# Four graph layers on one core: one chunk of edges in some units fetched row by row by SyncE

## The chip, the cores and the metric

The kernel runs on one core of a Trainium2 chip, as one program. Its time is device time in microseconds (us), from start to end of one execution. Engines are named as in the profile: PE is TensorE, DVE is VectorE, ACT is ScalarE, POOL is GpSimd, SP is SyncE, which does no arithmetic on tiles: it issues DMAs, loads registers and waits. "SPq" and "POOLq" are the sequencers' own instructions.

## The reference, cut to what matters

A graph of 12,500 nodes with 128 features and 212,500 edges, sorted by their target node `dst`, passes through four layers, each added to its input `x`. Every layer reads, for each edge, the row of its source node `src`, and reduces over the edges of a target.

```python
h = relu(layernorm(x));  x = x + L0(h)      # two graph attention layers
h = relu(layernorm(x));  x = x + L1(h)      # a transformer layer over the edges, with a feed-forward block
h = relu(layernorm(x));  x = x + L2(h)      # L2, the maximum:
#   msgs = h[dst] @ Wd + h[src] @ Ws + edge_weight * ww + bm
#   agg  = segment_max(msgs, dst);  out = relu(h @ W1a + agg @ W1b + b1) @ W2 + b2
h = relu(layernorm(x));  x = x + L3(h)      # L3, the last sum:
#   segment_sum(h[src], dst) / max(count(dst), 1)
```

## The kernel before, in words

Edges are cut into chunks of 128 (`P`), one edge to a partition: 1661 chunks (`CH`). Nodes are cut into 98 tiles of 128 (`T`). A *unit* is 17 chunks (`U`); unit u goes with tile u, whose edges lie in its 17 chunks and three more on either side. After a preparation of about 160 us there are five passes over all 98 units (`edge_pass`): `gat1`, `gat2`, `attn`, `max` and `sum`. The classes `gat`, `attn`, `maximum` and `total` (the sum, which inherits from `maximum`) say what each does.

In every pass a table of node rows lies in DRAM (`ts_` for the maximum, 128 float32 to a row; `th` for the sum, 129). `Pass.gather` (L1206 to L1214) fetches the rows of a group of up to three chunks: POOL issues one indirect DMA for each chunk, which reads 128 indices from a column of the tile `IDX` and brings 128 rows to 128 partitions. A unit has six groups, the last one of two chunks, so 17 indirect DMAs. In the sum the gathered rows go straight to PE, which multiplies a one-hot matrix (`se`, cast to `sef` by ACT on L1258) with them and adds into `acc` (L1267); in the maximum they are first transposed and run through a scan along the sorted edges (`e1`).

The order of the work is written out by hand: `edge_pass` keeps a calendar `cal` of rounds, 24 to a unit (`RU`), and in each round takes one step of every generator that is live, sorted by a rank. Each engine carries out its own instructions in that order. A round is an order, not a time. The gather of group i of unit u stands 24 rounds before round 24 u + 4 i, its first use (`e1`) at round 24 u + 4 i.

SP's program in a pass is a list in the same order: in the sum, for each unit, the store of a result tile `out_x<-o`, which waits for DVE, and the loads of `x`, `se` and `gt`; in the maximum the store `xd<-x`, three loads of `w`, one of `n0`, the store `th<-h`, and the loads of `gt`, `x` and `fa`. Every DMA of SP raises one of eight semaphores in turn, and in the built program a DMA waits for the one issued eight before it on SP.

In the preparation the generator `prepared` makes `IDX` by transposing `sd`, the source numbers in float32 (`chunks`, L291 to L298), and afterwards the tile `ch`, which marks where a new target begins.

Of the kernel before, what the change touches and what calls it, by code (L numbers as in the profile page):

```python
# [65 lines left out]
def gnn_kernel(ctx, tc, a, out):  # L66
# [17 lines left out]
    ww_d = dram.tile([3, D], BF16, name="ww_d")  # L84
    feat_d = dram.tile([T, 5, EW], BF16, name="feat_d")
    last_d = dram.tile([T, 5, EW], BF16, name="last_d")
    ewf_d = dram.tile([3, CP * P], BF16, name="ewf_d")
    first_d = dram.tile([1, (CP + 16) * P], BF16, name="first_d")
    xd = dram.tile([NP, D], F32, name="xd")
# [198 lines left out]
    def chunks(out, x, on):  # L288

        o = out.rearrange("p (r b) -> p r b", b=RC)  # L290
        for b0 in range(0, RC, 4):  # L291
            n = min(4, RC - b0)
            px = psum([P, 4, P], "b", "px")
            for b in range(n):
                PE.transpose(px[:, b, :], x[:, (b0 + b) * P:(b0 + b + 1) * P], ident)
            yield
            on(o[:, :, b0:b0 + n].rearrange("p r b -> p b r"), px[:, :n, :])
# [108 lines left out]
    def prepared(wp):  # L406
        tn_i = wp.tile([P, 1], I32, name="tn_i")
        GP.iota(tn_i, pattern=[[0, 1]], base=0, channel_multiplier=P)
        tid = wp.tile([T, 1], I32, name="tid")
        GP.iota(tid, pattern=[[0, 1]], base=0, channel_multiplier=1)  # L410
        tn = wp.tile([P, 1], F32, name="tn")
        V.tensor_copy(tn, tn_i)
        tn1 = wp.tile([P, 1], F32, name="tn1")
        V.tensor_scalar_mul(tn1, tn, -1.0)
        tn2 = wp.tile([P, 1], F32, name="tn2")
        V.tensor_scalar_add(tn2, tn, float(P))
        yield

        w = rd_[:, 1:EW + 1]
        eq = wp.tile([T, EW - P], BF16, name="eq")
        long_ = wp.tile([T, 1], F32, name="long_")
        V.scalar_tensor_tensor(eq, w[:, P:], 0.0, w[:, :EW - P], op0=ALU.add, op1=ALU.is_equal,
                               accum_out=long_)
        yield
        f = wp.tile([T, 2], F32, name="f")
        V.tensor_scalar(f[:, 0:1], rd_[:, 0:1], tn[:T, :], long_, op0=ALU.is_ge, op1=ALU.max)
        V.tensor_scalar(f[:, 1:2], rd_[:, EW + 1:], tn2[:T, :], f[:, 0:1], op0=ALU.is_lt,  # L430
                        op1=ALU.max)
        V.tensor_scalar_min(f[:, 1:2], f[:, 1:2], 1.0)
        yield
        p2 = psum([P, P], "mm", "p2")
        PE.transpose(p2[:1, :T], f[:, 1:2], ident[:T, :T])
        yield
        flag = wp.tile([1, T], F32, name="flag")
        V.tensor_copy(flag, p2[:1, :T])
        zr = wp.tile([1, T], F32, name="zr")
        V.memset(zr, 0.0)  # L440
        ord_ = wp.tile([1, T], F32, name="ord_")
        V.tensor_tensor_scan(ord_, flag, zr, 0.0, op0=ALU.add, op1=ALU.add)
        V.tensor_copy(NOV, ord_[:, T - 1:T])

        at = wp.tile([1, T], F32, name="at")
        V.scalar_tensor_tensor(at, flag, -float(2 * T), ord_, op0=ALU.mult, op1=ALU.add)
        V.tensor_scalar_add(at, at, float(2 * T - 1))
        yield
        pfl = psum([P, P], "mm", "pfl")
        PE.matmul(pfl[:, :T], ones[0:1, :], flag, start=True, stop=True)  # L450
        p3 = psum([P, P], "mm", "p3")
        PE.transpose(p3[:T, 0:1], at, ident[0:1, 0:1])
        yield
        V.tensor_copy(FLAG, pfl[:, :T])
        at_i = wp.tile([T, 1], I32, name="at_i")
        V.tensor_copy(at_i, p3[:T, 0:1])
        GP.indirect_dma_start(out=list_d, in_=tid, in_offset=None,
                              out_offset=bass.IndirectOffsetOnAxis(ap=at_i[:, 0:1], axis=0),
                              bounds_check=T - 1, oob_is_err=False)
        SY.dma_start(LIST, list_d.rearrange("(p t) c -> p (t c)", p=1))  # L460
        yield

        yield from chunks(IDX, sd, V.tensor_copy)

        ch = wp.tile([P, RC * P], F32, name="ch")
        V.tensor_tensor(ch, dd[:, 1:], dd[:, :RC * P], ALU.not_equal)
        yield
        yield from chunks(FIRST, ch, S.copy)
        m = wp.tile([P, RC * P], BF16, name="m")
        S.mul(m, ch, -BIG)  # L470
        SY.dma_start(first_d[0, P:(CP + 1) * P].rearrange("(p f) -> p f", p=P), m)
        yield
        dl = w
        V.tensor_scalar(dl, w, tn1[:T, :], FAR, op0=ALU.add, op1=ALU.min)
        V.tensor_scalar_max(dl, dl, -1.0)
        yield
        xb = wp.tile([T, EW], BF16, name="xb")
        S.copy(xb, dl)
        SY.dma_start(feat_d[:, 2, :], xb)
        hi, lo = yield from square(wp, dl, [T, EW], "q")  # L480
        for k, y in ((3, hi), (4, lo)):
            SY.dma_start(feat_d[:, k, :], y)
        yield
# [648 lines left out]
    def last_rows(pool):  # L1132
# [9 lines left out]
        for c0 in range(0, EW, n):  # L1142
# [30 lines left out]
                SY.dma_start(last_d[:, k, c0:c0 + n], y)  # L1173
            yield

    class Pass:


# [10 lines left out]

        made, whole = True, True  # L1190

        def __init__(self):
            self.rhs, self.gs, self.f, self.fa, self.x, self.n0 = {}, {}, {}, {}, {}, {}
            self.st, self.se, self.acc = {}, {}, {}

# [6 lines left out]
        def x_load(self, t):  # L1202
            if self.source is not None:
                self.x[t] = features(self.source, t, self.width)
            yield

        def gather(self, u, i):
            c, n = groups_of(u)[i]
            g = self.pool.tile([P, GS, self.wid], self.dt, name="g", bufs=self.bufs)
            for j in range(n):  # L1210
                k = u * U + c + j
                GP.indirect_dma_start(  # L1212
                    out=g[:, j, :], out_offset=None, in_=self.table,
                    in_offset=bass.IndirectOffsetOnAxis(ap=IDX[:, k:k + 1], axis=0))  # L1214
            self.gs[u, i] = g
            yield
# [81 lines left out]
    def edge_pass(name, table, wid, dt, wids, work_of, post, extra=()):  # L1298
        nonlocal ps_now
        w = work_of  # L1300
        with tc.tile_pool(name=name, bufs=2) as pool, \
                tc.tile_pool(name="ps_" + name, bufs=1, space=PSUM) as pp, tc.manual_schedule():
            ps_now, w.pool, w.table, w.wid, w.dt, w.wids = (pp, w.banks), pool, table, wid, dt, wids
            cal = {}

            def at(r, rank, g):
                cal.setdefault(r, []).append((rank, g))

            for u in range(T):
                r0 = u * RU  # L1310
                at(r0 - RU, 0, w.load(u))
                at(r0 + RU - 4 - w.tail[0] * (u == T - 1), 0, w.load2(u))
                for i, _ in enumerate(groups_of(u)):
                    at(r0 - RU + i * RG, 0, w.gather(u, i))
                    at(r0 + i * RG, 5, w.e1(u, i))
                    if w.e2_at is not None:
                        e2_at = w.e2_at if u < T - 2 else w.e2_last or w.e2_at
                        at(r0 + e2_at[i] - w.tail[0] * (u == T - 1), 4, w.e2(u, i))
                if w.chain_at is not None:
                    at(r0 + w.chain_at - w.tail[0] * (u == T - 1), 3, w.chain(u))  # L1320
                n = len(w.batches(u))
                rt = r0 + w.tile_at
                loads = rt - RU
                rt -= w.tail[1] * (u == T - 2) + w.tail[2] * (u == T - 1)
                at(min(loads, rt + RU - 9 - 3 * (n - 1) - 2), 0, w.tile_load(u))
                at(rt, 0, w.x_load(u))
                for b in range(n):
                    at(rt + RU - 9 - 3 * (n - 1 - b), 2, w.batch(u, b, n))
                at(rt + RU - 4, 1, w.ends(u, post))
            for g in extra:  # L1330
                at(0, 1, g(pool))
            live, r = [], min(cal)
            while live or cal:
                live += cal.pop(r, [])
                live.sort(key=lambda g: g[0])
                live = [g for g in live if next(g[1], live) is not live]
                r += 1
# [116 lines left out]
        V.tensor_tensor(c, x, b, ALU.subtract)  # L1454

    class gat(Pass):
        chain_at, e2_at, tile_at = RU + 5, range(RU + 13, 2 * RU + 1, 2), 2 * RU

        def __init__(self, c, source=None):
# [116 lines left out]
            return r  # L1576

    class attn(Pass):
        bufs, source, width = 17, x2d, 2 * D
        chain_at, tile_at = RU + 7, 2 * RU + 2  # L1580
        e2_at = [RU + 15 + r for r in (0, 2, 4, 6, 7, 11)]
# [68 lines left out]
            return r  # L1650

    class maximum(Pass):
        feats, bufs, source, made = last_d, 20, xd, False
        tile_at, tail = 12, (0, 0, 8)
        banks = {"pm": 1, "x": 2, "acc": 1, "pg": 2, "mm": 2}
# [45 lines left out]
            return r  # L1701

    class total(maximum):
        bufs, made = 24, True
        tile_at, tail = 10, (0, 0, 0)
        banks = {"acc": 2, "mm": 2}
# [173 lines left out]
```

## Time and profile before

| | |
|---|---|
| three runs | 10796.43, 10801.2 and 10809.79 us; median 10801.2 |
| the profiled execution | 10801.08 us, span 10799.4 us |
| busy in the span | POOL 7916.2 us (73%), PE 7520.8 (70%), ACT 4675.5 (43%), DVE 4569.7 (42%) |
| indirect DMAs issued by POOL (L1212) | 8305: 3322 in the two attention passes of the first layer, 1661 in each of the other three |
| mean of one in the maximum, in the sum | 944 ns, 947 ns |
| granted TensorE clock | 0.722 of full speed |

The page of the profile lists busy time by engine, the span in 40 slices, the DMA queues, the chain of work that ended last, and the costliest groups of instructions, each with its count, mean duration, and the idle time of its engine before it with what ended that idle time. The sequencers' instructions, DMA issues among them, are not counted as busy: SP stands in no row of the page, and is seen in the timeline alone, where each issue has a start and a duration.

### The profile page before, as it was taken

Reading aid. Unit: us, or ns where it says so; the run is one execution under the profiler, and the core shown is the slowest. Engines: PE = TensorE matmul, PEld = TensorE weight load, DVE = VectorE, ACT = ScalarE, POOL = GpSimd, SP = SyncE. Lnnn points to the kernel's source line nnn. Section 1 sums busy time; section 2 is a strip of 40 time slices with the busy share of each in tenths; the row PEclk is TensorE's granted clock in tenths of the full one; section 3 lists DMA queues with packets and bytes.
Section 4 is the critical chain, followed back from the end, with each engine's and each line's share of the span. In section 5 each row is a group of like instructions: output and inputs, shape, how many; then the busy total and the mean of one; then the engine's idle time right before and its main releaser. Section 6 shows DMA issues by size and latency. Waiting matters only on the chain. (4 is left out here: it accounts for less than half of the span.)

```text
span 10799.4 us, 149821 instructions
## 1 busy us (share of the span) xinstructions
PE 7520.8 (70%) x47184; PEld 5604.3 (52%) x47185; DVE 4569.7 (42%) x15187; ACT 4675.5 (43%) x13171; POOL 7916.2 (73%) x8330
## 2 busy tenths in 40 slices
PE   3676666656555556677777777888888866666666
PEld 2343333334444444566666666666666644444444
DVE  4555555544444444577777774333333310000000
ACT  4666666644444444355555554344434421111111
POOL 3777777767777777677777775777777767777777
PEclk6555555556677676799999998889888865555555
DMA  4222222224444444455555553333333323333333
GB/s 135 77 74 74 72 73 74 73 80 118 117 114 118 117 114 118 129 167 164 164 167 164 167 162 103 94 96 96 93 96 97 94 76 81 81 79 81 81 79 79
DMA packets 758382, 1143.66 MB, mean 106 GB/s; under 512 B 224040, under 2 KB 491511, under 8 KB 757471
## 3 DMA queue, kind: packets, MB, share of 16 engines
q0 software_dynamic: 292368, 610.29, 22.7%
q1 hardware_dynamic: 463932, 519.87, 14.9%
q8 instruction: 374, 6.13, 0.2%
q10 hardware_dynamic: 1268, 3.77, 0.1%
q14 instruction: 440, 3.60, 0.1%
HBM read 964.76 MB, written 168.43 MB: 105 GB/s over the span
## 5 line engine op out<-in xcount | busy, mean ns | idle before, releaser
L1212 POOL DMA_INDIRECT g<-t,IDX x3322 | 3156.3, 950 | 1173.2 <-issue 693.2
L1267 PE MATMUL acc<-xf,sef 128*128 128x131 f32 (+2 forms) x13458 | 2285.9, 320 | 563.3 <-ACT sef L1258 536.4
L1267 PEld LDWEIGHTS acc<-xf,sef 128*128 128x128 f32 x13458 | 1980.0, 222 | 736.1 <-ACT sef L1258 599.9
L1212 POOL DMA_INDIRECT g<-tkv,IDX x1661 | 1607.2, 968 | 547.5 <-issue 407.6
L1212 POOL DMA_INDIRECT g<-ts__83,IDX x1661 | 1568.6, 944 | 564.6 <-issue 359.1
L1212 POOL DMA_INDIRECT g<-th,IDX x1661 | 1572.3, 947 | 531.2 <-issue 409.0
L1267 PE MATMUL acc<-g,sef 128*128 128x129 f32 x4486 | 1360.2, 444 | 726.5 <-DMA g<-th,IDX 615.1
L1267 PEld LDWEIGHTS acc<-g,sef 128*128 128x128 f32 x4486 | 995.8, 302 | 1090.9 <-DMA g<-th,IDX 742.4
L1258 ACT CAST sef<-se 128x512 f32<-128x512 fp8e4 (+1 forms) x1755 | 1028.5, 598 | 438.1 <-PE acc L1267 432.5
L1282 DVE COPY_PREDICATED r<-FLAG,gt 128x129 f32<-128x129 int32 (+2 forms) x490 | 146.7, 299 | 2140.0 <-ACT r L1288 2076.6
L1683 DVE TENSOR_TENSOR_SCAN fm<-n,fm,pg 128x384 f32<-128x384 bf16 (+1 forms) x585 | 566.6, 969 | 935.0 <-PE pg L1680 933.7
L1495 PE MATMUL ex<-ADX,st 128*128 128x6 bf16 x4486 | 354.1, 174 | 835.2 <-ACT st L1109 372.2
L1495 PEld LDWEIGHTS <-st 128*128 128x128 fp8e4 x4486 | 328.7, 113 | 1005.3 <-ACT st L1109 565.3
L1500 ACT COPY lg<-g 128x3 f32<-128x3 f32 (+1 forms) x1172 | 226.6, 193 | 1142.0 <-DMA g<-t,IDX 1074.4
L1288 ACT COPY r<-acc 128x129 f32<-128x129 f32 (+2 forms) x392 | 105.9, 270 | 1308.0 <-PE acc L1267 1308.0
L1693 ACT COPY xf<-pt_f 128x384 f32<-128x384 f32 x586 | 270.6, 462 | 867.5 <-PE pt_f L1689 850.0
L1267 PE MATMUL acc<-xs,se 128*128 128x201 bf16 x2243 | 483.7, 368 | 229.6 <-ACT x L1553 118.1
L1124 PE MATMUL pm_se<-NF,fa 5*128 5x128 bf16 x4486 | 586.2, 266 | 0.0
L1418 DVE TENSOR_TENSOR_SCAN fw<-n,lt 17x384 f32<-17x384 bf16 (+1 forms) x294 | 303.2, 1031 | 545.4 <-PE lt L1430 545.4
L1109 ACT ACTIVATE st<-pm_st,ones 128x384 fp8e4<-128x384 f32 (+2 forms) x877 | 471.3, 537 | 121.1 <-PE pm_st L1116 121.1
L1613 PE MATMUL qe<-q,st 128*128 128x128 bf16 x6729 | 482.9, 222 | 23.8 <-DVE g L1618 16.7
L1689 PE MATMUL pt_f<-ident,fm 128*128 128x128 f32 x1661 | 342.5, 318 | 206.6 <-DVE xf L1692 141.4
(1098 smaller groups left out, 12350.4 us busy)
## 6 DMA issues: line engine op xcount, KB each, us to landing
se<-se_d SPq DMA_DIRECT2D x294, 368.0 KB
st<-st_d SPq DMA_DIRECT2D x196, 368.0 KB
g<-t,IDX POOLq DMA_INDIRECT x3322
n<-first_d SPq DMA_DIRECT2D x97, 544.0 KB
st_d<-st SPq DMA_DIRECT2D x98, 368.0 KB
se_d<-se SPq DMA_DIRECT2D x98, 368.0 KB
g<-tkv,IDX POOLq DMA_INDIRECT x1661
g<-ts__83,IDX POOLq DMA_INDIRECT x1661
```

The lines of the kernel that those rows point to most:

```text
L1109: S.activation(out, pm[:, :out.shape[1], :], AF.Relu, scale=-1.0, bias=ones[:, 0:1], saturate=False)
L1124: PE.matmul(pm[:, j, :], f[:, (c + j) * P:(c + j + 1) * P], NF, start=True, stop=True)
L1212: GP.indirect_dma_start(out=g[:, j, :], out_offset=None, in_=self.table, in_offset=bass.IndirectOffsetOnAxis(ap=IDX[:, k:k + 1], axis=0))
L1258: S.copy(se, self.se[t][:, at, :])
L1267: PE.matmul(acc[:, :m], se[:, j, :], x[:, i, :], start=(b == 0 and j == 0), stop=(b == n - 1 and j == len(ws) - 1))
L1418: V.tensor_tensor_scan(fw[:, s0 * P:(s0 + n) * P], n0[:, s0 * P:(s0 + n) * P], lt[:r, :n, :].rearrange("p j e -> p (j e)"), fw[:, s0 * P - ...
L1495: PE.matmul(ex[:, 6 * k:6 * k + 6], st, ADX[:, t, :, :].rearrange("p s v -> p (s v)"), start=(first and c0 == 0), stop=(stop and c0 + n - ...
L1500: S.copy(lg[:, 0, 1 + c0:1 + c0 + n, :], self.gs[u, i][:, :n, c + 1:c + 2])
L1613: PE.matmul(qe[0][:, k - c0, :], st, self.q[t][:, s * D:(s + 1) * D], start=(first and s == 0), stop=(stop and s == 2))
L1683: V.tensor_tensor_scan(fm[:, :m, :].rearrange("p j e -> p (j e)"), self.n0[u][:, cols], pg, self.prev, op0=ALU.add, op1=ALU.max)
L1689: PE.transpose(pt[:, j, :], fm[:, j, :], ident)
L1693: S.copy(ft[:, :m, :D], pt[:, :m, :])
```

## The change

`maximum` has `by_row = 3` and `total` has `by_row = 2`. In every third unit of the maximum (32 units) and every second of the sum (48 units), POOL issues 16 indirect DMAs, and the rows of the unit's 17th chunk come in another way. SP loads the chunk's 128 source numbers from a new DRAM list `src_x` into a small tile `rw`, loads them into registers 16 at a time, and issues for each a DMA of one row, whose address in the table is computed from the register. The rows go to the second half of a tile `gx` of two chunks; POOL's gather of the 16th chunk goes to its first half. These steps are spread over 64 rounds of 72 in the maximum (two rows in a round) and 40 of 48 in the sum (three or four in a round), and end 12 rounds after the unit's first round. The built program has, for each such chunk, one load of `rw`, 8 register loads, 128 register operations (three fused into one instruction each) and 128 DMAs on SP.

The list `src_x` is written once in the preparation, through the tile `ch`, whose allocation moves up.

```diff
+    src_x = dram.tile([CP * P, 1], I32, name="src_x")
...
+        ch = wp.tile([P, RC * P], F32, name="ch")
+        V.tensor_copy(ch.bitcast(I32), sd)
+        SY.dma_start(flat(src_x), ch.bitcast(I32))
+        yield
         yield from chunks(IDX, sd, V.tensor_copy)
 
-        ch = wp.tile([P, RC * P], F32, name="ch")
...
+    RR = 16
+    row_regs = [SY.alloc_register(f"row{i}") for i in range(RR)]
...
+        def row_units(self):
+            if self.by_row is None:
+                return [], 0
+            span = self.by_row * RU - 4
+            return [(u, RU // 2 - span) for u in range(T - 1) if u % self.by_row == self.by_row - 1
+                    and u * RU + RU // 2 - span >= -RU], span
+
+        def fetch_rows(self, u, span):
+            g = self.gx[u] = self.pool.tile([P, 2, self.wid], self.dt, name="gx", bufs=2)
+            rw = self.pool.tile([1, P], I32, name="rw", bufs=2)
+            e0 = (u * U + U - 1) * P
+            SY.dma_start(rw, src_x[e0:e0 + P, :].rearrange("(o f) c -> o (f c)", o=1))
+            for r in range(4):
+                yield
+            q = 0
+            for r in range(span - 4):
+                while q < P and q * (span - 4) < (r + 1) * P:
+                    if q % RR == 0:
+                        SY.load(row_regs, rw[0:1, q:q + RR])
+                    v = SY.snap(row_regs[q % RR], min_val=0, max_val=NP - 1)
+                    SY.dma_start(g[q:q + 1, 1, :], self.table[ds(v, 1), :])
+                    q += 1
+                yield
+
         def gather(self, u, i):
             c, n = groups_of(u)[i]
-            g = self.pool.tile([P, GS, self.wid], self.dt, name="g", bufs=self.bufs)
+            by_row = i == NG - 1 and u in self.gx
+            if by_row:
+                g, n = self.gx.pop(u), n - 1
+            else:
+                g = self.pool.tile([P, GS, self.wid], self.dt, name="g", bufs=self.bufs)
...
+            units, span = w.row_units()
+            for u, r in units:
+                at(u * RU + r, -1, w.fetch_rows(u, span))
...
     class maximum(Pass):
+        by_row = 3
...
     class total(maximum):
+        by_row = 2
```

More of the change, by code (lines that the diff above doesn't have):

```diff
@@ L1190, in gnn_kernel @@
         made, whole = True, True
+        by_row = None
         def __init__(self):
+            self.gx = {}
             self.rhs, self.gs, self.f, self.fa, self.x, self.n0 = {}, {}, {}, {}, {}, {}
@@ L1456, in gnn_kernel @@
     class gat(Pass):
+        by_row = None
         chain_at, e2_at, tile_at = RU + 5, range(RU + 13, 2 * RU + 1, 2), 2 * RU
@@ L1578, in gnn_kernel @@
     class attn(Pass):
+        by_row = None
         bufs, source, width = 17, x2d, 2 * D
```

## The prediction

> **What bounds the kernel now.** I read the page first, then the busy time in the stretches of the maximum and of the sum, then the gathers' line in the sum, POOL's timeline there, and at last the timeline and the waits of SP, which the page does not show.
>
> Part 1 of the page:
>
> ```profile
> PE 7520.8 (70%) x47184; PEld 5604.3 (52%) x47185; DVE 4569.7 (42%) x15187; ACT 4675.5 (43%) x13171; POOL 7916.2 (73%) x8330
> ```
>
> POOL at 73% does not look like a bound. The gathers' line in the sum's stretch and POOL's timeline there say otherwise:
>
> ```profile
> L1212 POOL DMA_INDIRECT g<-th,IDX x1661: 940/944/1064, 8713.8 to 10790.9; - x185
>   issue: 409.0, 1260
> ```
> ```profile
> 9000.29 0.94 POOL L1212 DMA_INDIRECT g<-th,IDX  x1 [0.30 <-issue]
> 9001.54 0.94 POOL L1212 DMA_INDIRECT g<-th,IDX  x1 [0.30 <-PE acc L1267]
> 9002.79 0.94 POOL L1212 DMA_INDIRECT g<-th,IDX  x1 [0.30 <-issue]
> ```
>
> One gather starts every 1.249 us, busy 0.94 and then 0.30 idle with nothing to wait for, and 1661 x 1.249 = 2075 us is the whole pass (8713.8 to 10791.8). The windows of the two passes, with PE's, PEld's, DVE's, ACT's and POOL's busy us, clock and DMA share:
>
> ```profile
> 6614.00:8690.00 2076.00, 1787.10 (x11560) 1328.31 (x11560) 805.39 (x2227) 829.78 (x1938) 1568.46 (x1661) 0.89 0.33 95
> 8714.00:10792.00 2078.00, 1358.95 (x4482) 995.01 (x4482) 95.46 (x388) 347.91 (x682) 1572.04 (x1661) 0.57 0.31 80
> ```
>
> Both passes last 98 units of 21.2 us = 17 gathers of 1.249 us, whatever PE and DVE do in them. So a gather less on POOL is worth 1.249 us, as long as nothing else becomes late. What is asked to do the work in its place is SP. Its timeline in one unit of the sum:
>
> ```profile
> 9104.91 0.34 SPq L919 DMA_DIRECT2D out_x<-o  x1
> 9105.29 0.43 SPq L712 DMA_DIRECT2D x<-xd  x1
> 9105.82 0.38 SPq L1229 DMA_DIRECT2D se<-se_d  x1
> 9106.24 0.43 SPq L1274 DMA_DIRECT2D gt<-gen_d  x1
> 9125.09 0.34 SPq L919 DMA_DIRECT2D out_x<-o  x1
> ```
>
> Four issues, 1.58 us and four gaps of some 0.045 us: 1.76 us of 21.2. The rest is a wait for the next result (DVE o), 1889.6 us in all in the pass:
>
> ```profile
> SPq L919 <- DVE o L917: 1889.6, 97, 27.0
> ```
>
> In the maximum a unit has nine issues (`xd<-x` 0.32, three of `w` 0.92, `n0` 0.34, `th<-h` 0.34, `gt` 0.43, `x` 0.48, `fa` 0.27), with gaps 3.5 us.
>
> **What it removes.** 32 + 48 = 80 gathers: 80 x 1.249 = 100 us of POOL.
>
> **What it adds on SP.** For each chunk: 128 one-row DMAs, 128 fused register operations, 8 register loads, one load of `rw`. No instruction of SP overlaps its neighbour in the timeline, so they add up. One-row loads from DRAM of 512 and 516 bytes, with constant addresses, are in the trace:
>
> ```profile
> 26.99 0.25 SPq L143 DMA_DIRECT2D w_bo<-in_L_gnn_bo  x1
> 27.29 0.29 SPq L576 DMA_DIRECT2D brow<-in_L_gnn_bf  x1
> 162.17 0.29 SPq L1150 DMA_DIRECT2D lrd<-dst_e  x1
> ```
>
> Starts follow ends by 0.04 to 0.05 us. A fused operation of three register steps and a load of one register stand on L943:
>
> ```profile
> L943 SPq TENSOR_LOAD <-NOV x4: 271/274/521, 162.8 to 170.1; - x4
> L943 SPq FUSED_REGOPS  x4: 147/147/159, 163.4 to 170.4; - x4
> ```
>
> One row then costs 0.15 + 0.29 + two gaps of 0.045 = 0.53 us, and 128 rows 67.8 us. That no issue with a register address was measured leaves both ends open: 0.215 us (the shortest issue, `nf_d` on L310) with 0.147 and gaps of 0.04 gives 0.442 us, 56.6 us in all; 0.43 us (what a 128-row load such as `x<-xd` takes to issue) gives 0.67 us, 85.8 us. I take 0.53, because lrd on L1150 is the same transfer but for the address. Register loads: 8 x (0.5 + 0.045) = 4.4 us, between 2.6 (0.274 each, if sixteen cost as one) and 8 x 16 x 0.274 = 35 us (if each register costs as a load of its own); I am near the lower end because the instruction is one. The load of `rw`: in the sum nothing stands between it and the register load that needs it, and the semaphore records of one-row loads land 1.2 to 2.4 us after issue, so 2.0 us (1.2 to 2.5).
>
> In the Trainium skill, DMA: Bandwidth & Descriptors, "Latency and other measured facts" puts the floor of a `tensor_load` at about 600 ns; the trace has 271 to 549 ns, so the trace decides. By the page's figure the eight loads would take 8 x 0.645 = 5.2 us (an estimate), 0.8 us more in each of the 80 chunks, 64 us in all.
>
> **Sum, per two units:** rows 67.8 + register loads 4.4 + `rw` 2.0 + SP's own eight issues 3.5 + the semaphore instructions some 0.4 = 78.1 us. Available: 42.4 us as it is, 41.2 with a gather gone. SP becomes the bound: 78.1 - 42.4 = +35.7 us, 48 times = **+1714 us**. The saving of POOL is off the path then.
>
> **Maximum, per three units:** 67.8 + 4.4 + 2.0 + 10.5 + 0.8 = 85.5 us against 63.6: +21.9, 32 times = **+701 us**. That the issue fills SP's wait for `xd<-x` (1439.6 us before) is counted: only what exceeds the unit's time is added.
>
> **Who waits.** In SP's order the loads of `se`, `x`, `gt`, `w`, `n0`, `fa` and the stores stand between rows, so each comes late by the rows ahead of it; PE then waits for the rows of `gx` and for `se`, DVE for `gt`, and POOL for free buffers of `g`. The eight semaphores cost nothing extra: eight rows take 4.2 us (at the low end of 0.442, 3.5), a row lands in 1.2 to 2.4; only behind `se`, which lands in about 3.5 us, can a row be held for a moment. The slack between the last row (round 12 of a unit) and its use (round 20 of the maximum, 25 of the sum) is some ten rounds; it hides a delay once, and not a rate.
>
> There is a rule that speaks the other way: the same page, "Issuing engines are not separate DMA queues", says that issuing from several engines only saves the sequencer's time, which is usually small relative to the DMA itself. The row above is 0.29 us of issue for a transfer that lands in 1.2 to 2.4 us, small for one alone; but up to eight are in flight, and 128 issues are not small. If issue were free, the sum would be 10801 - 100 = 10701 us (an estimate from the rule).
>
> **Preparation:** a cast of 128 x 1664 (0.99 us on L352) and a store as `src_e<-sd`, issued in 1.18 us; DVE's write into `ch` on L466 waits for that store, which for `src_e` landed 5.5 us after issue, with some 7 us of other DVE work between. 1 to 6 us, I take 3.
>
> **Sum:** 10801 + 1714 + 701 + 3 = 13219, taken as 13200 us. The base is the profiled execution, 10801.08 us with a span of 10799.4, 0.1 us from the median of the three runs.
>
> **The rivals.**
>
> *SP has room (faster).* If a row costs up to (41.2 - 2.6 - 1.2 - 3.5 - 0.4) / 128 = 0.26 us with its register step, SP keeps up in the sum; the maximum allows 0.37. Then POOL's 100 us are the result: 10801 - 100 + 3 = 10704 us. For it: SP idles over 90% of the sum now. Against it: a constant-address issue alone already takes 0.25 to 0.29 and a gap. Chance 0.07.
>
> *The register step is hidden under the issue.* A row costs 0.29 + 0.045 = 0.335 us: 42.9 + 7.7 = 50.6 us per two units of the sum, +8.2 x 48 = +394; the maximum takes 42.9 + 15.1 = 58.0 of 62.3 us and keeps its 32 x 1.249 = 40 us. 10801 + 394 - 40 = 11155 us. Against it: on L943 the register step begins where the load has ended (162.8 + 0.52, then 163.4), and the instruction after it begins at 163.6, where the step has ended: nothing overlaps. Chance 0.07.
>
> *Register loads go register by register.* 35 us instead of 4.4 in each chunk: 80 x 30.6 = +2448 over the forecast, 15670 us. For it: nothing in the trace loads more than one; against it: one instruction, one wait. Chance 0.05.
>
> **How the numbers follow.** The forecast, SP-bound with rows of 0.442 to 0.67 us, holds 0.80. Low end: sum 56.6 + 2.6 + 1.2 + 3.5 + 0.4 = 64.3, +21.9 x 48 = 1051; maximum 56.6 + 2.6 + 1.2 + 10.5 + 0.8 = 71.7, +8.1 x 32 = 259: 12111 us. High end: 96.1, +53.7 x 48 = 2578; 103.5, +39.9 x 32 = 1277: 14656 us. The three rivals hold 0.19, and 0.01 is for no change. The range of 11900 to 14700 takes the forecast's ends and a little below, and leaves the rivals out. Within 0.2% of the time before (21 us; about what a measurement can tell) lies almost nothing: it would need a row of just over 0.26 us. Faster 0.07, same 0.01, slower 0.92.
>
> **What the profile after would show.** If I am right: SP busy throughout both passes, with one-row issues about 0.53 us apart in its timeline and a FUSED_REGOPS between any two; SP's wait for DVE o nearly gone; the sum near 3790 us and the maximum near 2780 long; POOL's busy share down in both, its idle time ended by PE and by buffers. The other passes keep their 2104, 2137 and 2118 us. Rows 0.26 us apart or less, SP still waiting for DVE o, and a sum of some 2018 us would prove me wrong; so would rows at 0.53 us apart in a sum that is no longer, which would mean that SP's instructions overlap.

## The result, and the profile after

The changed kernel takes 12823.52 us (median of four runs, 12821.21 to 12838.43), the kernel before 10799.36 us (median of four, 10796.43 to 10809.79): 1.1878 times as long, 95% interval 1.1863 to 1.1893, 2024 us more. The forecast was 13200 us, with a range from 11900 to 14700.

Part 4 of the page before gives the chain of work that ended last by engine, and SP (as SPq) stands in it with nothing:

```profile
PE 11%; DMA 10%; POOL 9%; issue 6%; DVE 1%; ACT 1%; POOLq 0%; ACTq 0%; SPq 0%; DVEq 0%
```

Part 1 of the page of the kernel after, and the two rows of its chain that ended last (by engine, then by line):

```profile
PE 7071.0 (55%) x47184; PEld 5467.0 (43%) x47185; DVE 4575.0 (36%) x15188; ACT 4677.4 (36%) x13171; POOL 7839.1 (61%) x8250
...
SPq 27%; issue 9%; PE 8%; DMA 2%; DVE 1%; ACT 0%; DVEq 0%; ACTq 0%
SPq L1241 17%; SPq L1239 4%; SPq L1240 3%; PE acc L1309 3%; DMA gt<-gen_d 1%; PE pt_f L1737 1%; PE pg L1726 1%; PE pm_se L1129 1%; DVE fm L1731 1%; SPq L1714 1%; PE pg L1728 1%; PE pm L884 0%; DMA rw<-src_x 0%; PE ph L895 0%; SPq L924 0%
```

No engine is busier than 61%, and the engine at the head of the chain is one that part 1 does not list. Three lines of the new code, the row's DMA (L1241), the register load (L1239) and the register step (L1240), hold 24% of the span; POOL's gathers, 9% of the chain before, are gone from it.

The windows of the five passes (columns as in the prediction: length, busy us of PE, PEld, DVE, ACT and POOL, clock, DMA share, GB/s):

```profile
171.00:2275.00 2104.00, 1382.30 (x8135) 780.06 (x8136) 1138.31 (x4729) 1341.22 (x4541) 1572.81 (x1652) 0.50 0.29 74
2278.00:4415.00 2137.00, 1243.84 (x7561) 992.51 (x7560) 886.06 (x3287) 952.45 (x3149) 1581.10 (x1668) 0.69 0.40 114
4451.00:6571.00 2120.00, 1601.00 (x14726) 1393.70 (x14727) 1520.29 (x4026) 1075.26 (x2567) 1609.66 (x1661) 0.96 0.56 164
6625.00:9366.00 2741.00, 1851.29 (x11307) 1386.34 (x11308) 795.21 (x2181) 812.50 (x1895) 1537.47 (x1629) 0.77 0.25 72
9430.00:12824.00 3394.00, 807.10 (x4486) 768.42 (x4486) 96.00 (x392) 352.87 (x683) 1523.76 (x1613) 0.59 0.19 50
```

The first three passes are as long as before. The maximum lasts 2741 us instead of 2076 (+665), the sum 3394 instead of 2078 (+1316), together +1981. Ten more come ahead of the first pass, whose first gather is at 171.5 us and not at 161.1; the other 33 lie between and behind the windows, most of them between the maximum and the sum (64 us, 24 before).

What SP does there is seen in the lines' own instructions (count, then shortest, median and longest ns, then the first and the last start):

```profile
L1241 SPq MOVE gx<-th x6144: 29/29/37, 9432.8 to 12801.9; - x199
L1241 SPq DMA_DIRECT2D gx<-th x6144: 224/227/294, 9432.9 to 12801.9; - x199
...
L1240 SPq FUSED_REGOPS  x10240: 44/44/60, 6631.2 to 12801.8; - x197
...
L1239 SPq TENSOR_LOAD <-rw x640: 1132/1226/1427, 6630.0 to 12792.8; - x160
```

The rows fill the sum from end to end: 12801.9 - 9432.8 = 3369 us for 48 chunks is 70.2 us for two units. And SP's waits in the sum's stretch (us in total, times, longest):

```profile
SPq L1239 <- DMA rw<-src_x: 66.0, 48, 1.9
SPq L924 <- DVE o L922: 15.5, 3, 6.9
```

The wait for DVE o, 1889.6 us before, is down to 15.5: SP is never done early. Who waits for SP instead, in the same stretch:

```profile
DVE r L1324 <- DMA gt<-gen_d: 3204.9, 95, 38.6
```
```profile
POOL gx L1254 <- DMA gx<-th: 890.1, 35, 26.8
```

DVE waits nearly the whole pass for `gt`, which stands behind rows in SP's list, and so comes only when SP gets there. POOL's gather of the 16th chunk waits for the row DMAs into the same tile `gx`: POOL, which set the pace, now stands behind SP.

### The profile page after: what moved, and what is told of

It reads as the page before. It is cut to its first block, busy times and chain, and to the rows that moved or that the text cites. A ratio compares the mean times of both kernels' runs of the same rounds, so it can differ in the third digit from the quotient of the medians.

```text
span 12824.1 us, 181803 instructions
## 1 busy us (share of the span) xinstructions
PE 7071.0 (55%) x47184; PEld 5467.0 (43%) x47185; DVE 4575.0 (36%) x15188; ACT 4677.4 (36%) x13171; POOL 7839.1 (61%) x8250
## 5 line engine op out<-in xcount | busy, mean ns | idle before, releaser
L1254 POOL DMA_INDIRECT g<-t,IDX x3322 | 3156.0, 950 | 1182.5 <-issue 700.5
L1309 PE MATMUL acc<-xf,sef 128*128 128x131 f32 (+2 forms) x13458 | 2321.6, 324 | 571.8 <-ACT sef L1300 543.9
L1309 PEld LDWEIGHTS acc<-xf,sef 128*128 128x128 f32 x13458 | 2017.2, 226 | 749.7 <-ACT sef L1300 609.5
L1254 POOL DMA_INDIRECT g<-ts__84,IDX x1597 | 1507.2, 944 | 1211.9 <-PE pg L1726 466.6
L1254 POOL DMA_INDIRECT g<-tkv,IDX x1661 | 1609.7, 969 | 546.4 <-issue 401.8
L1254 POOL DMA_INDIRECT g<-th,IDX x1565 | 1478.6, 945 | 736.9 <-issue 421.3
L1324 DVE COPY_PREDICATED r<-FLAG,gt 128x129 f32<-128x129 int32 (+2 forms) x490 | 145.7, 297 | 4100.2 <-DMA gt<-gen_d 4005.5
L1309 PE MATMUL acc<-g,sef 128*128 128x129 f32 x4102 | 737.3, 355 | 973.7 <-ACT sef L1300 961.6
L1309 PEld LDWEIGHTS acc<-g,sef 128*128 128x128 f32 x4102 | 703.6, 267 | 1004.1 <-ACT sef L1300 985.8
L1309 PE MATMUL acc<-gx,sef 128*128 128x129 f32 x384 | 107.4, 403 | 1613.9 <-DMA rw<-src_x 1014.8
L1309 PEld LDWEIGHTS acc<-gx,sef 128*128 128x128 f32 x384 | 85.7, 294 | 1622.3 <-issue 714.6
L1254 POOL DMA_INDIRECT gx<-th,IDX x48 | 45.2, 942 | 1122.7 <-DMA gx<-th 890.1
L1737 PEld LDWEIGHTS pt_f<-ident,fm 128*128 128x128 f32 x1661 | 221.5, 168 | 940.7 <-DVE xf L1740 844.4
```

The costliest lines, as they stand in the source:

```text
L1254: GP.indirect_dma_start(out=g[:, j, :], out_offset=None, in_=self.table, in_offset=bass.IndirectOffsetOnAxis(ap=IDX[:, k:k + 1], axis=0))
L1309: PE.matmul(acc[:, :m], se[:, j, :], x[:, i, :], start=(b == 0 and j == 0), stop=(b == n - 1 and j == len(ws) - 1))
L1324: V.copy_predicated(r[:, :w], FLAG[:, t:t + 1].to_broadcast([P, w]), self.gt[:, :w])
L1737: PE.transpose(pt[:, j, :], fm[:, j, :], ident)
```

## The experiments

The theory: SP issues its list one instruction after the other, and rows and register loads fill it; the rate of that list sets both passes. The rivals: the rate of the rows' DMAs or their landing, and the place of the rows in the list.

**One pass at a time.** `by_row` set to None in `maximum`, or in `total`:

```diff
     class maximum(Pass):
-        by_row = 3
+        by_row = None
```

> Only the sum fetches rows by SP (by_row of the maximum is None). Theory, SP's own time is the bound in each pass by itself: the sum's window stays at 3394 us as in the changed kernel, the maximum's goes back to 2076, so 12823 - (2741 - 2076) = 12160 us, between 12130 and 12180. Rival, that the loss in one pass depends on the other (a backlog of SP or late stores carried over): the sum's window would be shorter than 3340 us or the total off by more than 60 us.

> Only the maximum fetches rows by SP (by_row of the sum is None). Theory: maximum 2741 us, sum 2078, so 12823 - (3394 - 2078) = 11510 us, between 11480 and 11530. With the run of the sum alone it shows whether the two parts and the preparation (10 us) add up to the 2024 us. Rival as for the sum alone: more than 60 us off.

The sum alone took 12134.95 us, ratio 1.1231 (1.1209 to 1.1254); the maximum alone 11530.54 us, ratio 1.0672 (1.0651 to 1.0693). Against 10804.53 us in the same runs that is +1330 and +726, 2056 together, with the ten us of the preparation counted twice; the two parts add up to the whole within some 20 us, and neither hides the other.

**Rows without registers.** The rows are fetched from constant addresses, without register loads and register steps. They are not the rows of the edges, but the same 128 for every chunk; number, size and place in SP's list are the same.

```diff
-                    if q % RR == 0:
-                        SY.load(row_regs, rw[0:1, q:q + RR])
-                    v = SY.snap(row_regs[q % RR], min_val=0, max_val=NP - 1)
-                    SY.dma_start(g[q:q + 1, 1, :], self.table[ds(v, 1), :])
+                    SY.dma_start(g[q:q + 1, 1, :], self.table[97 * q:97 * q + 1, :])
```

> The same 10240 one-row DMAs into the same tiles at the same places of SP's order, but at constant addresses of the table: no register loads and no register steps; the rows fetched are not those of the edges. Theory, SP's instructions add up: a row costs 0.228 + 0.045 = 0.273 us, two units of the sum 35 + 0.3 + 3.5 + 0.4 = 39.2 us against 41.2 of POOL, three of the maximum 46.6 against 62.3; so SP keeps up, both passes are POOL's again with 80 gathers less, and the time is 10800 + 10 - 100 = 10710 us, between 10690 and 10790. Rival, the landings bound (eight semaphores, or one-row transfers queued in one DMA engine): the DMAs are all still there, so the sum stays near 3394 and the total over 12500 us.

It took 11289.25 us, ratio 1.0441 (1.0424 to 1.0459): 1534 of the 2024 us are gone with the register work, while all 10240 DMAs remain. So three quarters of the loss is the register work, and the landing of the rows is not what holds the changed kernel at 12824 us. But neither of the two expected figures came out. Its rows:

```profile
L1238 SPq DMA_DIRECT2D gx<-th x6144: 214/251/457, 9166.3 to 11272.4; - x199
L1238 SPq DMA_DIRECT2D gx<-ts__84 x4096: 214/250/402, 6624.1 to 9100.0; - x196
```

An issue takes 0.25 us and, with its gap, some 0.295. The sum's rows last 2106 us, some 1.4% over the pass before: SP is just full there (128 x 0.295 + 3.5 = 41.3 us of 42.4, and rows held behind `se` for 78.8 us in the pass). The maximum's last 2476 us, 400 more than that pass took before, though its list has 128 x 0.295 + 10.5 = 48.3 us of work for 63.6. SP's waits in the maximum:

```profile
SPq L907 <- DVE st L693: 768.5, 94, 13.1
SPq L1238 <- DMA n<-first_d: 160.0, 95, 2.7
```

SP idles for 768.5 us before the store `xd<-x` (L907), and for 160.0 us more with a row that waits behind `n`, and the pass is late all the same. There the rate of the list is not the bound.

**Larger register loads.** 32 registers to a load instead of 16:

```diff
-    RR = 16
+    RR = 32
```

> 32 registers at a time, so 4 register loads for a chunk and not 8. The load of 16 took 1.23 us and 0.2 us of gaps, the load of one 0.27 in the kernel before. If a load costs by the register (0.27 + 0.063 for each further one), one of 32 takes 2.24 us and a chunk saves 8 x 1.43 - 4 x 2.44 = 1.7 us: 80 x 1.7 = 135 us, 12690 us. If it costs by the instruction, it saves 4 x 1.43 = 5.7 us: 460 us, 12365 us. If neither loads nor rows are on the path, 12823 us stay.

It took 12722.34 us, ratio 1.1775 (1.1752 to 1.1799): 101 us less. The load's line:

```profile
L1239 SPq TENSOR_LOAD <-rw x320: 2025/2118/2286, 6627.6 to 12685.7; - x160
```

From 1 to 16 to 32 registers, 0.271, 1.226 and 2.118 us: about 0.06 us for each further register (0.955 / 15 = 0.064, 0.892 / 16 = 0.056). A load costs by the register. The Trainium skill (DMA: Bandwidth & Descriptors, "Latency and other measured facts") gives a floor of some 600 ns for it. Here one register took less than that (0.271 us), and sixteen took twice as much.

**Fewer row units.** `by_row` 5 and 4, which leaves SP room at the measured prices: in the maximum some 85 us of work in five units of 21.2 (106 us; SP's own issues are 17.5 of it), in the sum some 74 in 84.8 (own issues 7).

```diff
     class maximum(Pass):
-        by_row = 3
+        by_row = 5
...
     class total(maximum):
-        by_row = 2
+        by_row = 4
```

> by_row 5 in the maximum and 4 in the sum: 19 + 24 chunks by SP. Theory: SP needs 54 + 11 + 2 us for a chunk, with its own issues 74 us for four units of the sum against 83.5, and for five of the maximum 54 + 11 + 2 + 17.5 + up to 13 of waits = 98 against 104.7; so SP keeps up and POOL's saving shows: 43 x 1.249 = 54 us less, 10 us more in the preparation, 10799 - 44 = 10755 us (10735 to 10790). Rival, that loads and stores which come late behind rows hold up PE and POOL even where SP has time to spare: 10800 us or more.

It took 11022.39 us, ratio 1.0191 (1.0177 to 1.0206). Its gathers (POOL's instructions on L1254):

```profile
L1254 POOL DMA_INDIRECT g<-ts__84,IDX x1623: 938/944/1059, 6621.6 to 8860.4; - x181
L1254 POOL DMA_INDIRECT g<-th,IDX x1613: 938/944/1062, 8951.3 to 10994.9; - x180
```

The sum did what was expected: 2044 us from first to last gather against 2077 before, 33 us less for 24 gathers (24 x 1.249 = 30). With room on SP, a gather taken from POOL is worth its price. The maximum did not: 2239 against 2074 us from first to last gather, and the sum's first gather follows 91 us later, 26 before, so that the pass costs 230 us more. SP waits 611.9 us at L907 in it, and DVE, at its copy of `gt` (L1324), waits for that load in 90 units:

```profile
SPq L907 <- DVE st L693: 611.9, 93, 10.1
```
```profile
DVE r L1324 <- DMA gt<-gen_d: 344.3, 90, 6.0
```

In the kernel before, SP waited longer at the same store, but DVE's copy had its `gt` early and waited for ACT alone:

```profile
SPq L902 <- DVE st L688: 1439.6, 96, 18.9
```
```profile
DVE r L1282 <- ACT r L1288: 127.6, 97, 1.7
```

No other DMA holds PE, DVE, ACT or POOL for more than some 20 us in this pass of the spaced kernel, but for one wait of 58.9 us at its start, which the kernel before has too. So the rows, `w`, `n` and `x` are in time, and `gt` is not. One unit in SP's timeline:

```profile
7501.57 0.35 SPq L907 DMA_DIRECT2D xd<-x  x1
7502.12 1.90 SPq L1241 DMA_DIRECT2D gx<-ts__84  x5
7504.07 0.87 SPq L1714 DMA_DIRECT2D w<-ewf_d  x3
7504.99 0.34 SPq L1716 DMA_DIRECT2D n<-first_d  x1
7505.43 0.39 SPq L913 DMA_DIRECT2D th<-h  x1
7506.02 5.30 SPq L1241 DMA_DIRECT2D gx<-ts__84  x9
7511.37 0.36 SPq L1316 DMA_DIRECT2D gt<-gen_d  x1
...
7525.03 0.35 SPq L907 DMA_DIRECT2D xd<-x  x1
```

Between the store and the load of `gt` lie 9.8 us of SP's list, 14 rows among them; 13.7 us after `gt` the next store goes out. In the kernel before, `gt` follows the store after some 3.55 us:

```profile
7508.54 0.32 SPq L902 DMA_DIRECT2D xd<-x  x1
...
7512.10 0.43 SPq L1274 DMA_DIRECT2D gt<-gen_d  x1
```

The proposal: the list is part of a loop. `gt` starts a chain on other engines that ends in the tile which the next `xd<-x` stores; SP waits for it at the head of its list, and the next `gt` comes after that. What SP issues between store and `gt` lengthens the loop, however much it idles elsewhere. From the units inside the pass, without its first and last few (medians, read from the starts of the two issues; the period is the mean):

| | store to `gt` | `gt` to store | period |
|---|---|---|---|
| before | 3.55 us | 17.38 us | 21.22 us |
| spaced (5 / 4) | 9.90 | 13.87 | 23.66 |
| constant rows | 11.28 | 14.51 | 26.04 |
| after | 13.96 | 14.27 | 28.62 |

From `gt` to the store it takes 13.9 to 14.5 us in all three of the others, and the period grows with the first column: 2.0 us until DVE's copy starts, which it does as soon as `gt` is there, and some 12 us of work on DVE, PE and ACT behind it. In the kernel before, where POOL sets 21.2 us, the copy starts 5.9 us after the issue of `gt`, and the same 14.3 us would leave the loop some 3 us of slack (21.2 - 3.55 - 14.3).

**The list written out last in the preparation.** As spaced, with `src_x` stored at the end of `prepared` through another tile:

```diff
-        V.tensor_copy(ch.bitcast(I32), sd)
-        SY.dma_start(flat(src_x), ch.bitcast(I32))
-        yield
...
+        V.tensor_copy(ed_.bitcast(I32), sd)
+        SY.dma_start(flat(src_x), ed_.bitcast(I32))
+        yield
```

> As the run spaced 5 and 4, but the list of sources is written at the end of the preparation through the tile of edge weights, so DVE's write into ch waits for no store. Theory: the 10 us of the preparation (DVE waited 9.3 us for the store of src_x) go down to 1 or 2: 8 us less than the run before, 10747 us. Rival, that the preparation's end is set by SP's or ACT's own work and not by that wait: no difference.

It took 11016.47 us, ratio 1.0183 (1.0169 to 1.0198). In the trace the first gather moves from 170.6 to 162.2 us (161.1 before), which accounts for the preparation's share; between the medians, 6 us apart, the runs' spread hides it.

**`gt` loaded early.** To test the loop: the load of `gt` goes some 20 rounds ahead, so that it no longer stands behind the rows.

```diff
         def x_load(self, t):
+            if self.gt_early:
+                self.gt_load(t)
...
-            gt = self.pool.tile([P, XW], F32, name="gt")
-            SY.dma_start(gt[:, :self.wids], gen_d[rows(t), :self.wids])
-            self.gt = gt
+            if not self.gt_early:
+                self.gt_load(t)
+            self.gt = self.gts.pop(t)
```

The edit was made to the kernel after, to spaced with the late list, to the kernel before, and to the constant rows.

> The changed kernel, with the load of gt moved in the maximum and the sum from the end of a tile to the load of its x, 20 rounds earlier in SP's order. Theory: in the maximum SP goes round a loop of its own: it issues gt, DVE's predicated copy waits for it, and some 14 us of chain later SP waits for that chain at the store xd<-x, with rows queued behind it (265 us of such waits in the pass). With gt early the waits go, and three units cost SP its instructions alone: 54 + 11 + 2 + 10.5 + 0.8 = 78 us instead of 84; 32.7 x 6 = 190 us less, 12630 us (12560 to 12690). Rival, that SP waits at xd<-x because PE and POOL are late on their own: the waits and 12823 us stay.

> The run spaced and late (5 and 4, the list written at the end of the preparation) with gt early. Theory: the maximum, which took 2240 us instead of 2076, loses its loop, SP has room in both passes, and POOL's 43 gathers show: 10800 + 1 - 54 = 10747 us (10730 to 10785). Rival, that the one-row transfers or the late rows slow the maximum in another way: 10800 us or more, up to the 11016 of the run without gt early.

> The kernel before with gt early and no rows by SP: a control. Theory: POOL's gathers bound both passes, SP's waits at xd<-x cost nothing there, so 10800 us, within 0.3%. Rival, that the earlier gt is a gain by itself: 10770 us or less.

> The rows at constant addresses (not those of the edges), every third and second unit, with gt early. A row took 0.295 us there. Theory: the sum stays where it was, 2112 us, since SP is full in it (128 x 0.295 + 4.2 = 42 us for two units); the maximum, 2490 us before this, falls to POOL's pace of 2036 us, as SP needs 128 x 0.295 + 11.6 = 50 of 62.3 us for three units: 11289 - 454 = 10835 us (10800 to 10900). Rival, that one-row landings hold up the maximum: 11200 us or more.

These four, and both repeats below, ran on other chips than the experiments so far; there the kernel before itself takes 14953.66, 15037.99 and 15126.17 us, so that only ratios within a chip can be read. The kernel after with early `gt`: 17824.48 us, 1.1915 (1.1893 to 1.1937); spaced: 15832.92, 1.0575 (1.0561 to 1.059); before: 14967.84, 1.0007 (0.9997 to 1.0016); constant rows: 15597.33, 1.0426 (1.0407 to 1.0445).

Early `gt` by itself costs nothing there. In the kernel after, SP's waits at L907 fall from 265.0 us to some 30 in the maximum; but its rows last 3123 us there and not 2734, so that SP is late anyhow, and this is no evidence for the loop. In spaced and in constant rows over 600 and 800 us of such waits stay. The ratios do not fall, and what sets the passes on these chips is not what sets them on the first. The gathers of the kernel before with early `gt`, and then of spaced with early `gt`:

```profile
L1219 POOL DMA_INDIRECT g<-ts__83,IDX x1661: 941/947/1065, 9815.2 to 12414.0; - x185
L1219 POOL DMA_INDIRECT g<-th,IDX x1661: 939/947/1046, 12495.8 to 14917.6; - x185
```
```profile
L1261 POOL DMA_INDIRECT g<-ts__84,IDX x1623: 939/947/1052, 9816.6 to 12497.0; - x181
L1261 POOL DMA_INDIRECT g<-th,IDX x1613: 941/947/962, 12582.7 to 15759.5; - x180
```

A gather takes 947 ns as ever, but the passes without rows last 2599 and 2422 us and not 2075: POOL waits for other engines (PE above all, 383 and 235 us in the two passes of the first of the two kernels), so a gather less need not shorten a pass. Spaced is 82 us longer in the maximum and 755 in the sum, the pass where it gained on the first chip. SP's timeline there shows why:

```profile
14000.05 9.32 SPq L1248 DMA_DIRECT2D gx<-th  x9
14010.06 0.70 SPq L924 DMA_DIRECT2D out_x<-o  x1
14011.49 0.69 SPq L1248 DMA_DIRECT2D gx<-th  x1
14012.89 0.71 SPq L1217 DMA_DIRECT2D gt<-gen_d  x1
14014.29 0.01 SPq L717 DMA_DIRECT2D x<-xd  x1
14015.68 0.70 SPq L1278 DMA_DIRECT2D se<-se_d  x1
14017.78 32.22 SPq L1248 DMA_DIRECT2D gx<-th  x34
14050.10 0.38 SPq L924 DMA_DIRECT2D out_x<-o  x1
14050.68 0.23 SPq L1248 DMA_DIRECT2D gx<-th  x1
14050.97 0.36 SPq L1217 DMA_DIRECT2D gt<-gen_d  x1
```

From 14010 to 14016 us five issues start 1.4 us apart, and the waits that the profile has for SP there make 0.4 us; from 14050 the first three of them start some 0.3 to 0.6 us apart. In such stretches SP's own instructions come at less than half their pace, which costs most where its list is long.

> The same kernel as e8 once more: e7 to e10 ran on another chip, on which the kernel before takes 14954 us, POOL waits for other engines in every pass and its gathers no longer set the pace, so they say nothing of a saving on POOL. On a chip where the kernel before takes 10800 us, theory: the maximum loses its loop through gt, and POOL's 43 gathers show, 10747 us (10730 to 10785). Rival, that late rows or one-row transfers slow the maximum in another way: 10800 us or more, up to the 11016 of e6.

> The kernel of e8 and e11 once more, for a chip on which the kernel before takes about 10800 us. If SP's list makes the maximum's delay (gt loaded early no longer waits behind the rows that SP issues between xd and gt): the maximum's pass returns from 2240 us (e5) to about 2045 to 2076, and the whole to about 10760 to 10850. If the maximum's delay has another cause: the pass stays near 2240 and the whole near 11016 (e6).

Spaced with early `gt` ran twice more, on two more such chips: 16001.67 us, 1.0635 (1.0621 to 1.065), and 16059.55 us, 1.0617 (1.0599 to 1.0634). Whether early `gt` frees the maximum where POOL sets the pace stays open. With constant rows and early `gt` the maximum's gathers lasted 2652 us, 53 more than without rows, where constant rows alone had cost 372 by the same measure on the first chip; but with a period of 26.5 us (2599 / 98) there, a loop of 25.8 us (11.28 + 14.51) would be covered anyhow, if its steps take as long there.

## Why the prediction was right, and where its steps were off

**What bounds the kernel.** Right: POOL's 1.249 us a gather set both passes. The sum of the spaced kernel gave 33 us for 24 gathers.

**A row on SP, 0.53 us.** In the sum 0.417 is the median from one row to the next, and 0.429 the mean, below the low end of 0.442. The register step takes 44 ns, not the 147 of L943, and the issue 0.227 us, not 0.29; a MOVE of 29 ns, which the prediction did not have, stands between them. With the medians of the gaps: 0.044 + 0.036 + 0.029 + 0.031 + 0.227 + 0.051. The step that failed is the choice of the neighbours: both rows belonged to other uses, and both were dearer. What makes the one on L943 longer was not tested.

**Register loads, 4.4 us a chunk.** A load between two rows puts them 1.284 us further apart: 8 x 1.284 = 10.3 us. The reason given (one instruction, so near the lower end) is refuted by the load of 32; the rival of loads that go register by register was right in kind, at 0.06 us a register and not 0.274. (The 271 to 549 ns that the prediction gives for the loads of the kernel before leave out one of 556 ns, on DVE.)

**The list for two units of the sum, 78.1 us.** Rows 54.9 (128 x 0.429), loads 10.3, `rw` 1.6, own issues with their semaphores 3.5 make 70.3; the profile has 70.2. The pass grew by 1316 us where 1714 were forecast: rows forecast 12.9 us too dear and loads 5.9 us too cheap, for two units, are nearly the whole difference.

**The maximum, 85.5 us for three units.** 2734 / 32 = 85.4, but not for the reason given, and that it came so close is luck. With measured prices the list holds 55.3 (128 x 0.432) + 10.4 + 1.6 + 10.4 = 77.7 us; the other 8 are waits, most of them at the store `xd<-x` (265.0 us in the pass):

```profile
SPq L907 <- DVE st L693: 265.0, 59, 8.9
SPq L1239 <- DMA rw<-src_x: 54.0, 32, 3.4
```

The step that failed is "the issue fills SP's wait for `xd<-x`". The wait is not free time to be filled in front of it: rows ahead of `gt` delay the work that it waits for. Taken as a rate alone, 77.7 us would have given some +450 instead of +665. That the list's rate is not the bound there, the constant rows and the spaced kernel show. That the loop is, rests on the table of periods and on the two waits that close it (DVE for `gt`, SP for what follows from it), and was not shown by taking it away.

**Who waits.** Right for `gt` (DVE), for `gx` (PE) and for `se` (ACT, which casts it, and PE behind ACT). Not foreseen: POOL waits for the rows themselves, 890.1 us in the sum. The semaphores cost nothing in the changed kernel: SP's waits in its sum show none for a row's landing.

**Preparation, 3 us (1 to 6).** 10 us in the trace, above the range: DVE's write into `ch` waited 9.3 us for the store of `src_x`, which the 7 us of other DVE work were to cover.

**The rivals.** SP has room: it needed 0.26 us a row in the sum, and even with registers gone a row takes 0.295. The register step hidden under the issue: it needed 0.335 us a row, and the steps do follow one another. Issue that is small beside the transfer, which the Trainium skill calls the usual case (DMA: Bandwidth & Descriptors, "Issuing engines are not separate DMA queues"), is not what was seen. It would have given 10701 us: 128 issues with their register work were 55 us, and the passes grew by 1981.

**Where the luck lies.** The direction, the bound in the sum and the range held by the mechanism. That the time came within 377 us of the forecast is in part luck: with the row as measured and every other term as forecast, the prediction's sum would have given some 12200 us, and the dearer loads and the waits in the maximum, neither of them foreseen, brought it up again.

## What to carry to other kernels

Work given to an idle queue costs its instructions one by one: count every register load, step, move and issue, times the gap, against the time of the unit, and take prices from rows of the same form, with both ends kept. Then ask what the queue itself waits for: if a load that it issues starts the work that its own later store waits for, everything put between store and load lengthens that loop, and its idle time there is not room. (Here the loop is argued from the waits and the periods, as said above.) The one form that gained here is the sum with one chunk in four, 33 us in its pass; the sum alone in that form was not run (some 10780 us, an estimate for the list written late: 10815 - 33).

## What the runs showed of the hardware

A register load from a tile costs 0.27 us for one register and about 0.06 us for each further one (1.226 us for 16, 2.118 for 32). A fused register step took 44 ns here and 147 ns on L943 of the kernel before. The same kernel took about 10800 us on one chip and 14954 to 15126 us on three others, with a gather at 944 and 947 ns: there the engines waited for one another, and in stretches SP's instructions started 1.4 us apart. What holds them up was not found.
